# Clearing the sorted rows of a mixture of experts: only past each expert's last token, or all of them beforehand

## The chip, the cores and the metric

The kernel runs on one core of one Trainium2 chip. The metric is the time of one execution on the device in microseconds (us); the median of several runs is compared. One further execution was taken with the hardware profiler; the profile's views (page, waits, timeline, stretches of time) are all of that one execution.

## The reference, cut to what matters

The program is two layers, each an attention part and a feed-forward part, over x of 16 batch rows x 256 tokens x 256 features. Three quarters of the work (a conditioning attention, an attention of 16 heads, a quantized feed-forward, a diffusion step and a second attention) come first. The last part is a mixture of experts:

```
def _L1_ffn_ref(x, w_router, W1, b1, W2, b2, Ws1, bs1, Ws2, bs2):
    # D_MODEL 256, D_FF 1024, N_EXPERTS 8, TOP_K 2, one shared expert
    logits = einsum('btd,ed->bte', x, w_router)
    vals, idx = top_k(softmax(logits), 2)
    gates = sum(one_hot(idx, 8) * vals[..., None], axis=-2)
    acc = einsum('btf,df->btd', gelu(einsum('btd,fd->btf', x, Ws1) + bs1), Ws2) + bs2
    h = gelu(einsum('btd,efd->btef', x, W1) + b1)
    y = einsum('btef,edf->bted', h, W2) + b2
    return SCALE * (acc + einsum('bted,bte->btd', y, gates))

x = x + attention0(cross_attention(x, fside, braak_embed[stage]))
x = x + fp4_feed_forward(x @ W[category] + b[category])
x = x + attention1(diffusion(x, zX, zY, zR))
x = x + _L1_ffn_ref(conditioned(x, expert_of_row), ...)
```

Each of the 4096 tokens goes to 2 of 8 experts, so 8192 rows are to be worked on by experts, in numbers that are known only at run time.

## The kernel before, in words

**Two parts.** `program` runs `setup`, then `woven`, then `mixture`.

**The woven part** (0 to about 1720 us) holds everything up to the second attention. It is written as 22 generators, `stage_a`, `stage_f`, `stage_d` and so on, each of which yields the instructions of one kind of work for batch rows 0 to 15. `weave` is a planner: it keeps a modelled time at which each engine comes free, and again and again issues, of the next instructions of all generators, the one that could start first by the model (ties go by the ranks in `ORDER`). The order in which it issues is the order in which each engine works. An instruction on SyncE (its queue is where the transfers are issued) is booked with 0.5 us of that engine, and a transfer's data counts as there 1.5 us (`MOVED`, from on-chip memory) or 3.2 us (`LANDING`) later. The generators hold each other back through flags in `g.done`. `stage_f` does the feed-forward of layer 0 for batch row b and then sets `done["F"]` to b + 1; `stage_d`, the diffusion that opens the second attention for row b, waits for that flag (L1079), and `stage_e`, once all 16 are done, loads what the mixture needs first (`fetch_c`).

In the second attention the rotated queries and keys are made by VectorE and GpSimd (`turned4`, tiles `f_t1q` and `f_t1k`) and moved to other partitions by four small transfers each (`f_q<-f_t1q`, `keys<-f_t1k`, 64 KB) on SyncE; TensorE then takes the scores from `keys` and `f_q` (`scores4`). Weights are loaded by `fetch_p` (`wq`) and `fetch_u` (`wv`), the inputs of the next row by `fetch_a`, all on SyncE.

**The mixture.** `conditioned` works in blocks of 512 tokens. For each block `route` finds the two experts of each token and its place within each expert's region, and scatters the token's row into `ysort`, an array in HBM, with 8 indirect transfers on GpSimd (64 in all, L1531). Expert e owns the rows from e x REGION x 256 on. After the last block, `plan_tiles` counts the tokens of each expert (`pc`), rounds the counts up to tiles of 256 rows and makes a table of which tile belongs to which expert. Then four blocks of the shared expert run (`shared_block`), and after them 35 tiles of 256 sorted rows (`expert_tiles`), each of which reads its rows (`ys<-ysort`, L1392) and its expert's weights on SyncE. The last 4 of 39 tiles run only if the counts need them. `combine` gathers the results with indirect transfers.

**What the change touches.** A tile may reach past its expert's last token, and a spare tile may have no tokens at all. So that these rows hold numbers, before the change all of `ysort` (8 x 16 x 256 rows of 1 KB, 32 MB) is filled with zeros from the tile `zero`: after each batch row, `stage_f` yields two writes of 1 MB on SyncE, and only then sets its flag.

Of the kernel before, what the change touches and what calls it, by code (L numbers as in the profile page):

```python
# [12 lines left out]
F32 = mybir.dt.float32  # L13
I32 = mybir.dt.int32
BF16 = mybir.dt.bfloat16
AF = mybir.ActivationFunctionType
ALU = mybir.AluOpType
AX = mybir.AxisListType

P = 128  # L20
S = 256
D = 256
# [6 lines left out]
NE = 8  # L29
# [4 lines left out]
OUT_SCALE = 1.0 / math.sqrt(1 + TOPK / NE)  # L34
TT = 256
SPARE = NE // 2
REGION = 16
MAGIC = 1.5 * 2.0**22


# [4 lines left out]
def mm(nc, out, pairs, start=True, stop=True):  # L45

    last = len(pairs) - 1
    for i, (lhsT, rhs) in enumerate(pairs):
        nc.tensor.matmul(out, lhsT, rhs, start=start and i == 0, stop=stop and i == last)  # L49


def bank(k):

    return k.ps.tile([P, 512], F32, name=f"bank{k.stream}", tag=f"bank{k.stream}")
# [8 lines left out]
def setup(ctx, tc, a, n_batch):  # L63
    nc = tc.nc
    k = Ctx()
    k.nc, k.tc, k.a, k.B, k.turn, k.stream = nc, tc, a, n_batch, False, 0
    k.const = ctx.enter_context(tc.tile_pool(name="const", bufs=1))
    c = k.const
    k.ident = c.tile([P, P], F32, name="ident")
    make_identity(nc, k.ident)  # L70

    k.mask = c.tile([P, 2 * P], F32, name="mask")
    nc.gpsimd.memset(k.mask[:, :P], 0.0)
    make_causal_mask(nc, k.mask[:, P:], mask_val=NEG)

    k.idx = c.tile([64, 3, n_batch], I32, name="idx")
    k.onehot = c.tile([16, n_batch], F32, name="onehot")


    k.n_tiles = (TOPK * n_batch * S + NE * (TT - 1)) // TT  # L80
    dram = ctx.enter_context(tc.tile_pool(name="dram", bufs=1, space=bass.MemoryType.DRAM))
    k.ysort = dram.tile([NE * REGION * TT, D], F32, name="ysort")
    k.osort = dram.tile([k.n_tiles * TT, D], F32, name="osort")
    k.zero = c.tile([P, D], F32, name="zero")
    nc.gpsimd.memset(k.zero, 0.0)

    k.xd = [dram.tile([S, D], F32, name=f"xd{b}") for b in range(n_batch)]
    return k
# [670 lines left out]


def stage_f(g):
    k, a = g.k, g.a
    regions = NE * REGION * TT // (2 * g.B)
    for b in range(g.B):
        yield lambda b=b: g.done["Y"] > b
        yield from feed_forward0(g, b)

        for i in (2 * b, 2 * b + 1):
            rows = k.ysort[i * regions : (i + 1) * regions, :].rearrange("(p r) d -> p r d", p=P)
            yield g.sp.dma_start(out=rows, in_=k.zero.unsqueeze(1).to_broadcast([P, regions // P, D]))  # L770
        g.done["F"] = b + 1


# [604 lines left out]
def expert_rows(k, pool, r, t):  # L1378

    k.stream = t % 2  # L1380
    nc, a = k.nc, k.a

    own = k.p2.tile([P, 10], F32, name="own_b1", tag="own_b1")
    b1, entry = own[:, 0:8], own[:, 8:10].bitcast(I32)
    nc.vector.tensor_copy(b1, r.b1t[:, t, :])
    nc.vector.tensor_copy(entry, r.table[:, :, t])
    e = nc.sync.value_load(entry[0:1, 0:1], min_val=0, max_val=NE - 1)
    row = nc.sync.value_load(entry[0:1, 1:2], min_val=0, max_val=(NE * REGION - 1) * TT)
    w1 = pool.tile([P, 2, FF1], F32, name="w1", tag="w1")
    w2 = pool.tile([P, 8, D], F32, name="w2", tag="w2")  # L1390
    ys = k.p2.tile([P, 2, D], F32, name="ys", tag="ys")
    nc.sync.dma_start(out=ys, in_=k.ysort[bass.ds(row, TT), :].rearrange("(c p) d -> p c d", p=P))  # L1392
    nc.sync.dma_start(out=w1, in_=a["w1"][bass.ds(e, 1)].rearrange("e p c f -> p (e c) f"))
    nc.sync.dma_start(out=w2, in_=a["w2"][bass.ds(e, 1)].rearrange("e p f d -> p (e f) d"))
    b2 = k.p2.tile([P, D], F32, name="eb2", tag="eb2")
    nc.sync.dma_start(out=b2, in_=a["b2"][bass.ds(e, 1)].to_broadcast([P, D]))
    ysT = k.p2.tile([P, 2, TT], F32, name="ysT", tag="ysT")
    transposed(
        k,
        ysT.rearrange("p c (s t) -> p (c s) t", t=P),  # L1400
        [ys[:, s, c * P : (c + 1) * P] for c in range(2) for s in range(2)],
    )
    return ysT, w1, w2, b1, b2
# [46 lines left out]
def routing_state(k, keep):  # L1450
# [23 lines left out]
    for e in range(NE):  # L1474
        nc.gpsimd.memset(r.base[:, e : e + 1], float(e * REGION * TT))
    r.tri = keep.tile([P, NE, NE], F32, name="tri")
# [59 lines left out]
            )  # L1536


def plan_tiles(k, keep, r):

    nc = k.nc
    NT, n = 2 * k.B, k.n_tiles
    pc = bank(k)[:, :NE]
    mm(nc, pc, [(r.all, r.seen[:, NT, :])])
    cnt = keep.tile([P, NE], F32, name="cnt")
    ci = keep.tile([P, NE], I32, name="cnt_i")
    nc.vector.tensor_scalar(cnt, pc, float(TT - 1), None, ALU.add)
    nc.vector.tensor_copy(ci, cnt)
    nc.vector.tensor_scalar(ci, ci, TT.bit_length() - 1, None, ALU.arith_shift_right)
    nc.vector.tensor_copy(cnt, ci)  # L1550
    tmp = keep.tile([P, NE, NE], F32, name="pl_tmp")
    first = keep.tile([P, NE], F32, name="pl_first")
    end = keep.tile([P, NE], F32, name="pl_end")
    nc.vector.tensor_tensor(tmp, r.tri, cnt.unsqueeze(1).to_broadcast([P, NE, NE]), ALU.mult)
    nc.vector.tensor_reduce(first, tmp, AX.X, ALU.add)
    nc.vector.tensor_tensor(end, first, cnt, ALU.add)
    for t in range(n - SPARE, n):
        rows = k.osort[t * TT : (t + 1) * TT, :].rearrange("(c p) d -> p c d", p=P)
        nc.sync.dma_start(out=rows, in_=k.zero.unsqueeze(1).to_broadcast([P, 2, D]))
    r.used = keep.tile([P, 1], I32, name="pl_used")  # L1560
    nc.vector.tensor_copy(r.used, end[:, NE - 1 : NE])

    nc.gpsimd.memset(end[:, NE - 1 : NE], float(n))
    idx = keep.tile([P, n], I32, name="pl_idx")
    nc.gpsimd.iota(idx, pattern=[[1, n]], base=0, channel_multiplier=0)
    t_ = keep.tile([P, n], F32, name="pl_t")
    nc.vector.tensor_copy(t_, idx)
    wide = [P, n, NE]
    tw = t_.unsqueeze(2).to_broadcast(wide)
    ew = lambda x: x.unsqueeze(1).to_broadcast(wide)  # L1570
    hot = keep.tile(wide, F32, name="pl_hot")
    low = keep.tile(wide, F32, name="pl_low")
    nc.vector.tensor_tensor(hot, tw, ew(end), ALU.is_lt)
    nc.vector.tensor_tensor(low, tw, ew(first), ALU.is_ge)
    nc.vector.tensor_tensor(hot, hot, low, ALU.mult)
    ids = keep.tile([P, NE], I32, name="pl_ids")
    nc.gpsimd.iota(ids, pattern=[[1, NE]], base=0, channel_multiplier=0)
    idf = keep.tile([P, NE], F32, name="pl_idf")
    nc.vector.tensor_copy(idf, ids)
    tab = keep.tile([P, 2, n], F32, name="pl_tab")  # L1580
    nc.vector.tensor_tensor(low, hot, ew(idf), ALU.mult)
    nc.vector.tensor_reduce(tab[:, 0, :], low, AX.X, ALU.add)

    off = keep.tile([P, NE], F32, name="pl_off")
    nc.vector.scalar_tensor_tensor(off, first, -float(TT), r.base, ALU.mult, ALU.add)
    nc.vector.tensor_tensor(low, hot, ew(off), ALU.mult)
    nc.vector.tensor_reduce(tab[:, 1, :], low, AX.X, ALU.add)
    nc.vector.scalar_tensor_tensor(tab[:, 1, :], t_, float(TT), tab[:, 1, :], ALU.mult, ALU.add)
    nc.vector.tensor_scalar(tab[:, 1, :], tab[:, 1, :], float((NE * REGION - 1) * TT), None, ALU.min)
    r.table = keep.tile([P, 2, n], I32, name="pl_table")  # L1590
    nc.vector.tensor_copy(r.table, tab)

    r.b1t = keep.tile([P, n, 8], F32, name="b1t")
    part = keep.tile([P, n, 8], F32, name="b1part")
    for e in range(NE):
        h = hot[:, :, e : e + 1].to_broadcast([P, n, 8])
        dst = part if e else r.b1t
        nc.vector.tensor_tensor(dst, h, k.b1[:, e, :].unsqueeze(1).to_broadcast([P, n, 8]), ALU.mult)
        if e:
            nc.vector.tensor_tensor(r.b1t, r.b1t, part, ALU.add)  # L1600

    nc.vector.tensor_scalar(off, first, float(TT), None, ALU.mult)
    nc.vector.tensor_tensor(r.rank, r.rank, off.unsqueeze(1).to_broadcast([P, NT, NE]), ALU.add)
    pos = keep.tile([P, TOPK, NT], F32, name="pos_f")
    for i in range(TOPK):
        nc.vector.tensor_tensor(r.hot[:, i], r.hot[:, i], r.rank, ALU.mult)
        nc.vector.tensor_reduce(pos[:, i, :], r.hot[:, i], AX.X, ALU.add)
    r.pos_o = keep.tile([P, TOPK, NT], I32, name="pos_o")
    nc.vector.tensor_copy(r.pos_o, pos)
# [182 lines left out]
```

## Time and profile before

| | |
|---|---|
| median of 3 runs | 2716.26 us (2714.77 to 2721.61) |
| the profiled execution | 2712.26 us |
| its span, first to last instruction | 2710.5 us |
| granted TensorE clock, mean | 0.985 |
| TensorE / VectorE / ScalarE / GpSimd busy | 96% / 48% / 45% / 36% |
| zero writes, first and last issue | 186.5 and 1632.2 us |
| transfers in all | 303.59 MB |

Engines are PE (TensorE), PEld (its weight load), DVE (VectorE), ACT (ScalarE), POOL (GpSimd) and SP (SyncE; SPq is its queue). In a timeline row stand the start, the duration, engine, line, operation, output and inputs, the number of instructions merged, and in brackets the idle time before it with what ended that. Every instruction of the woven part carries line L181, so there it is told apart by its tiles. In rows on a stretch of time stand the stretch, its length, the busy time of PE, PEld, DVE, ACT and POOL with instruction counts, the granted clock, the share of the 16 DMA engines that was busy, and GB/s.

### The profile page before, as it was taken

The numbers are of one execution on the slowest core, as the hardware profiler recorded it, in microseconds if no ns is written. First come the engines' busy times: TensorE is split into PE (matmuls) and PEld (weight loads), VectorE is DVE, ScalarE is ACT, GpSimd is POOL, SyncE is SP. The second block draws the span as 40 slices with busy tenths as digits, with TensorE's granted clock in tenths as the row PEclk, the third lists the DMA queues.
The fourth block names the chain that finished last, engine by engine and source line by source line (L and its number), as shares of the span: only waits on it lengthen the run. The fifth ranks groups of instructions, "written<-read, shape, count | busy, mean of one in ns | idle before, by whom it ended". The sixth has DMA issues, their size and how long they took to land. (4 is left out here: it accounts for less than half of the span.)

```text
span 2710.5 us, 39421 instructions
## 1 busy us (share of the span) xinstructions
PE 2593.2 (96%) x13569; PEld 1902.7 (70%) x13569; DVE 1310.9 (48%) x2557; ACT 1211.4 (45%) x3618; POOL 988.4 (36%) x1022
## 2 busy tenths in 40 slices
PE   8988999999999999999999998999999999999999
PEld 7755666766766666676776676555566888888866
DVE  6466666666677755766667664234330000000023
ACT  2554636655565654655655643333322222222321
POOL 5344544545555544554545543233320000000045
PEclk9999999999999998999999999999999999999999
DMA  4121233333333233233242336411120555655523
GB/s 123 52 87 50 90 115 114 93 117 108 94 111 109 67 113 115 69 118 124 80 124 89 89 114 185 135 52 47 49 103 1 185 195 192 204 186 192 194 86 109
DMA packets 249657, 303.59 MB, mean 112 GB/s; under 512 B 43120, under 2 KB 216432, under 8 KB 240112
## 3 DMA queue, kind: packets, MB, share of 16 engines
q1 hardware_dynamic: 243312, 284.26, 33.4%
q0 software_dynamic: 6144, 16.79, 2.0%
q8 instruction: 110, 1.80, 0.3%
q14 instruction: 91, 0.75, 0.1%
HBM read 206.85 MB, written 60.56 MB: 99 GB/s over the span
## 5 line engine op out<-in xcount | busy, mean ns | idle before, releaser
L181 PE MATMUL single<-e_zT,wq 128*128 128x256 f32 x1024 | 288.6, 403 | 8.3 <-DMA wq<-in_w_qk 7.5
L1436 POOL DMA_INDIRECT got<-osort,pos_o x64 | 62.2, 972 | 626.5 <-ACT hT L1369 584.9
L1418 ACT ACTIVATE ehT<-bank,own_b 128x256 f32<-128x256 f32 x280 | 132.5, 473 | 349.1 <-PE bank L49 349.1
L181 POOL TENSOR_TENSOR b_e<-b_e,b_stat 128x512 f32<-128x512 f32 (+1 forms) x128 | 189.7, 1483 | 179.1 <-DVE b_stat L181 167.4
L49 PE MATMUL bank<-ysT,w 128*128 128x256 f32 x1120 | 247.6, 379 | 0.2 <-ACT ysT L105 0.2
L49 PE MATMUL bank<-w,ehT 128*128 128x256 f32 x1120 | 247.5, 379 | 0.0
L49 PEld LDWEIGHTS bank<-ysT,w 128*128 128x128 f32 x1120 | 212.7, 190 | 29.4 <-ACT ysT L105 0.5
L49 PEld LDWEIGHTS bank<-w,ehT 128*128 128x128 f32 x1120 | 210.2, 190 | 27.2
L181 ACT ACTIVATE b_e<-b_e,b_stat 128x128 f32<-128x128 f32 (+1 forms) x512 | 227.0, 447 | 0.9 <-DVE b_stat L181 0.9
L181 PEld LDWEIGHTS single<-e_zT,wq 128*128 128x128 f32 x1024 | 178.8, 193 | 50.6 <-issue 15.2
L181 ACT ACTIVATE f_prob<-f_prob,f_stat 128x144 f32<-128x144 f32 x512 | 207.5, 410 | 12.1 <-DVE f_stat L181 12.1
L181 ACT COPY b_pT<-single 128x512 f32<-128x512 f32 x190 | 108.8, 588 | 138.2 <-PE single L181 137.4
L181 PE MATMUL pair<-keys,f_q 64*128 64x144 f32 x1024 | 126.8, 334 | 16.6 <-DMA keys<-f_t1k 13.1
L1426 DVE TENSOR_TENSOR eo<-bank,eb 128x512 f32<-128x512 f32 x35 | 24.2, 691 | 234.4 <-PE bank L49 234.4
L181 PE MATMUL single<-wv,e_zT 128*128 128x256 f32 x512 | 134.1, 386 | 2.7 <-DMA wv<-in_w_v 1.4
L181 PE MATMUL single<-wo,f_oT 128*128 128x256 f32 x512 | 131.4, 383 | 3.5 <-ACT f_oT L181 3.3
L181 PEld LDWEIGHTS pair<-keys,f_q 64*128 64x128 f32 x1024 | 77.0, 188 | 81.7 <-issue 60.8
L181 ACT COPY f_pT<-single 128x512 f32<-128x512 f32 x130 | 76.0, 588 | 122.9 <-PE single L181 120.4
L181 POOL TENSOR_TENSOR f_t1q<-f_t1q,f_t2q 128x256 f32<-128x256 f32 x128 | 93.0, 746 | 96.6 <-DVE f_t2q L181 65.1
L181 POOL TENSOR_TENSOR f_prob<-f_prob,f_stat 128x1024 f32<-128x1024 f32 x64 | 127.2, 1987 | 0.1
L181 PE MATMUL single<-ident,b_e 128*128 128x128 f32 x768 | 119.9, 285 | 7.2 <-POOL b_e L181 4.2
L1531 POOL DMA_INDIRECT ysort<-r_y,r_posi x64 | 62.4, 975 | 162.2 <-DMA ysort<-r_y,r_posi 103.6
(299 smaller groups left out, 5324.9 us busy)
## 6 DMA issues: line engine op xcount, KB each, us to landing
w<-in_w SPq DMA_DIRECT2D x70, 1024.0 KB, 5.3
wq<-in_w_qk SPq DMA_DIRECT2D x128, 256.0 KB, 3.3
ysort<-zero SPq DMA_DIRECT2D x32, 1024.0 KB, 7.3
wv<-in_w_v SPq DMA_DIRECT2D x64, 256.0 KB, 3.6
f_q<-f_t1q SPq DMA_DIRECT2D x256, 64.0 KB, 2.0
keys<-f_t1k SPq DMA_DIRECT2D x256, 64.0 KB, 2.1
wo<-in_w_out SPq DMA_DIRECT2D x64, 256.0 KB, 3.1
ys<-ysort SPq DMA_DIRECT2D x35, 256.0 KB, 2.7
```

The costliest lines, as they stand in the source:

```text
L49: nc.tensor.matmul(out, lhsT, rhs, start=start and i == 0, stop=stop and i == last)
L181: return Op([(self.name, self.cost(fn, outs, aps), lambda: call(*args, **kw))], outs, aps)
L1418: nc.scalar.activation(hT[:, f, :], ph, AF.Gelu_apprx_tanh, bias=b1[:, f : f + 1])
L1426: nc.vector.tensor_tensor(o, po, b2.unsqueeze(1).to_broadcast([P, 2, D]), ALU.add)
L1436: nc.gpsimd.indirect_dma_start(out=g, out_offset=None, in_=k.osort[:, :], in_offset=bass.IndirectOffsetOnAxis(ap=r.pos_o[:, i, t : t + 1], ...
L1531: nc.gpsimd.indirect_dma_start(out=k.ysort[:, :], out_offset=bass.IndirectOffsetOnAxis(ap=posi[:, i, t : t + 1], axis=0), in_=ys[t], in_of ...
```

## The change

The two writes per batch row in `stage_f` go, and `done["F"]` is set right after the feed-forward. In `plan_tiles`, as soon as the counts `pc` are there, the new `blank_rows` adds each expert's count to the start of its region, loads the eight sums into registers of SyncE one after the other, and from each of these rows on writes 256 rows of zeros (for the last expert 1024 rows). REGION grows from 16 to 17 and `ysort` gets 3 x 256 rows behind the last region, so that the writes stay inside; the bound on a tile's first row follows.

```diff
-REGION = 16
+REGION = 17
+PAST = 3
...
-    k.ysort = dram.tile([NE * REGION * TT, D], F32, name="ysort")
+    k.ysort = dram.tile([(NE * REGION + PAST) * TT, D], F32, name="ysort")
...
 def stage_f(g):
     k, a = g.k, g.a
-    regions = NE * REGION * TT // (2 * g.B)
     for b in range(g.B):
         yield lambda b=b: g.done["Y"] > b
         yield from feed_forward0(g, b)
-
-        for i in (2 * b, 2 * b + 1):
-            rows = k.ysort[i * regions : (i + 1) * regions, :].rearrange("(p r) d -> p r d", p=P)
-            yield g.sp.dma_start(out=rows, in_=k.zero.unsqueeze(1).to_broadcast([P, regions // P, D]))
         g.done["F"] = b + 1
...
-    row = nc.sync.value_load(entry[0:1, 1:2], min_val=0, max_val=(NE * REGION - 1) * TT)
+    row = nc.sync.value_load(entry[0:1, 1:2], min_val=0, max_val=(NE * REGION + PAST - 1) * TT)
...
+def blank_rows(k, keep, r, counts):
+
+    nc = k.nc
+    ends, endi = keep.tile([P, NE], F32, name="ends"), keep.tile([P, NE], I32, name="ends_i")
+    nc.vector.tensor_tensor(ends, counts, r.base, ALU.add)
+    nc.vector.tensor_copy(endi, ends)
+    for e in range(NE):
+        base, n = e * REGION * TT, TT + PAST * TT * (e == NE - 1)
+        row = nc.sync.value_load(endi[0:1, e : e + 1], min_val=base, max_val=base + (REGION - 1) * TT)
+        rows = k.ysort[bass.ds(row, n), :].rearrange("(p r) d -> p r d", p=P)
+        nc.sync.dma_start(out=rows, in_=k.zero.unsqueeze(1).to_broadcast([P, n // P, D]))
...
 def plan_tiles(k, keep, r):
...
     ci = keep.tile([P, NE], I32, name="cnt_i")
+    blank_rows(k, keep, r, pc)
     nc.vector.tensor_scalar(cnt, pc, float(TT - 1), None, ALU.add)
...
-    nc.vector.tensor_scalar(tab[:, 1, :], tab[:, 1, :], float((NE * REGION - 1) * TT), None, ALU.min)
+    nc.vector.tensor_scalar(tab[:, 1, :], tab[:, 1, :], float((NE * REGION + PAST - 1) * TT), None, ALU.min)
```

## The prediction, made before the change was run

> **What bounds the kernel now.** I read the page first, then who TensorE waited for, then the stretches of time in which the 32 writes run, and last the place where the new writes will stand.
>
> ```profile
> span 2710.5 us, 39421 instructions
> PE 2593.2 (96%) x13569; PEld 1902.7 (70%) x13569; DVE 1310.9 (48%) x2557; ACT 1211.4 (45%) x3618; POOL 988.4 (36%) x1022
> ysort<-zero SPq DMA_DIRECT2D x32, 1024.0 KB, 7.3
> keys<-f_t1k SPq DMA_DIRECT2D x256, 64.0 KB, 2.1
> ```
>
> TensorE is busy for 96% of the span and nothing else for half of it, so time can be won only where TensorE stands still or runs at a lower clock. The writes to be removed are 1 MB each, 32 times. The small moves of rotated keys, 64 KB each, share their queue.
>
> The waits of TensorE alone, longest first in total (who, for what: us, times, longest):
>
> ```profile
> PE pair L181 <- DMA keys<-f_t1k: 13.1, 4, 4.0
> PE single L181 <- DMA wq<-in_w_qk: 7.5, 1, 7.5
> PE pair L181 <- DMA wq<-in_w_qk: 3.4, 1, 3.4
> ```
>
> Only four of 256 key moves were waited for, and the timeline puts those waits at 362.3, 963.0, 1068.9 and 1273.6 us, each 7.7 to 10.3 us after the second of a pair of zero writes was issued. The queue of SyncE around the third of them:
>
> ```profile
> 1059.90 0.62 SPq L181 DMA_DIRECT2D keys<-f_t1k  x1
> 1060.57 1.32 SPq L181 DMA_DIRECT2D ysort<-zero  x2
> 1061.99 4.23 SPq L181 DMA_DIRECT2D keys<-f_t1k  x3
> 1066.32 2.29 SPq L181 DMA_DIRECT2D wq<-in_w_qk  x2
> ```
>
> Ahead of the pair an issue takes 0.62 us; behind it three take 4.23 us, 1.4 us each, and in this stretch the DMA view gives the keys 5.8 us to landing instead of 2.1. On TensorE:
>
> ```profile
> 1064.75 0.60 PE L181 MATMUL single<-e_zT,wq 128*128 128x256 f32 x2
> 1065.19 0.60 PE L181 MATMUL single<-ident,b_e 128*128 128x128 f32 x4
> 1068.93 0.52 PE L181 MATMUL pair<-keys,f_q 64*128 64x144 f32 x4 [3.15 <-DMA keys<-f_t1k]
> 1069.38 1.22 PE L181 MATMUL single<-e_zT,wq 128*128 128x256 f32 x2
> ```
>
> It waits 3.15 us, and then the same two matmuls take 1.22 us where they took 0.60. The stretches behind the waits, with the granted clock in the third column from the right, show why:
>
> ```profile
> 362.78:366.19 3.41, 3.41 (x12) 2.21 (x11) 2.40 (x4) 0.00 (x0) 1.06 (x1) 0.50 0.71 226
> 963.52:966.94 3.42, 3.42 (x12) 2.08 (x12) 1.56 (x5) 0.99 (x3) 1.66 (x3) 0.50 1.03 350
> 1069.34:1076.16 6.82, 6.82 (x22) 4.27 (x21) 1.65 (x5) 1.39 (x5) 1.75 (x3) 0.50 0.93 287
> 1274.14:1277.55 3.41, 3.41 (x5) 1.35 (x5) 0.00 (x0) 0.00 (x0) 0.00 (x0) 0.50 0.82 251
> 1646.19:1653.02 6.83, 3.52 (x8) 2.87 (x9) 0.00 (x0) 0.00 (x0) 0.00 (x0) 0.50 0.85 216
> ```
>
> After each of the waits the clock stands at 0.50 for 3.4 or 6.8 us. So such a wait costs itself and then half of the slow stretch.
>
> **Part one: the 32 writes leave the woven part.** Two writes per batch row go, each 0.66 us of SyncE's queue (21 us in all) and 1 MB of traffic. The queue time by itself is worth nothing, since SyncE is not the bound. What counts is who stood behind them.
>
> The four key waits: 3.12 + 2.83 + 3.15 + 3.99 = 13.1 us. Would the keys be in time without the pair? Third wait: GpSimd made the last of their rows at 1058.7 + 0.7 = 1059.4, the three issues would start at 1060.57, end at 1062.5, and land 2.1 us after the last began, at 1064.0; TensorE wanted them at 1065.8. The same working gives 1268.4 against 1269.6 for the fourth, 358.0 against 359.2 for the first and 955.8 against 960.1 for the second. All four vanish if the order stays.
>
> The slow clock behind them: 3.41 + 3.42 + 6.82 + 3.41 = 17.1 us at 0.50, so 8.5 us. The Trainium skill ("TensorE: Matmul & The Clock Gate", Part 1: The HAM clock gate) lets the clock fall to half after at least one idle window of about 3.4 us. By that rule three of these waits, at about 3 us, would leave the clock alone, and the gain would be 6.8 us smaller; the trace disagrees and shows 0.50 behind each.
>
> The last pair, at 1631.6, stands ahead of eight loads for the next stage, and then of the `wq` that TensorE waits 7.53 us for (until 1649.50); of the slow stretch there 3.52 us are worked, which costs 1.8. The gain lies between 0 (the eight loads clog the queue by themselves) and 9.3 us (the pair's 2 MB take about 8 us at the 260 to 300 GB/s of the other pairs' stretches). I take half, 4.6.
>
> Sum with the order kept: 13.1 + 8.5 + 4.6 = 26.2 us, at most 30.9.
>
> But the order won't be kept. `weave` books 0.5 us of SyncE for each of these writes, and `stage_f` sets `done["F"]`, which releases `stage_d`, only after them. Without them later DMAs are booked up to 1 us earlier, and the greedy choice goes another way from 187 us on. Between 200 and 1720 us TensorE's waits add up to 75.3 us, of which the zero writes explain 13.1 + 7.5; the other 55 us get drawn again. The 200 us stretches from 400 to 1600 us have 5.7 to 9.4 us without TensorE work, so a redraw moves one by 2 us or so either way, and all eight, if independent, by about 5. I set 4 us of the gain aside for it, because a TensorE that is held up less reaches the next late operand of ScalarE or GpSimd sooner. That leaves 22 us.
>
> **Part two: eight writes in `plan_tiles`.** Two VectorE operations on 128x8, like L1547's 0.15 us, enter at 1991 us. TensorE is then in 14 us of matmuls from 1997.7 and waits for no result of the plan, so they cost nothing; uncovered they would cost 0.3 us. SyncE gets eight register loads, each about 0.58 us by the reads of L1387 (0.27 for the load, 0.15 and 0.02 for what follows, the rest between them), and eight writes: seven of 256 KB and one of 1 MB. The skill ("DMA: Bandwidth & Descriptors", Latency and other measured facts) gives such a load a floor of about 600 ns; the trace shows 0.27, and by the page's figure SyncE would be busy some 2.6 us longer.
>
> The writes must wait for the last scatter, which the read of tile 0 already does:
>
> ```profile
> 2015.48 0.41 SPq L1392 DMA_DIRECT2D ys<-ysort  x1
> 2093.98 1.01 PEld L99 LDWEIGHTS bank<-ident,ys 128*128 128x128 f32 x8
> ```
>
> Queued behind them on SyncE are that read and the expert weights of tiles 0 and 1. TensorE meanwhile has shared blocks until 2094, 78 us of cover. If the eight don't wait for each other, SyncE needs 8 x (0.58 + 0.66) = 10 us and the last lands 5 to 12 us later: the read goes out near 2033. If each waits for the one before it, with 2.7 us to landing for 256 KB (the clearing of `osort`) and 7.3 for 1 MB, it is 7 x 3.3 + 7.9 = 31 us, so near 2047. The weights follow in 5 us and take at most 14.4 to land: 2067. Either way the cover holds and the price is 0. If it failed, each us beyond would stop TensorE. The scatters wait for each other (103.6 us of GpSimd) before and after; the clamp and the region size are constants and cost nothing.
>
> **The rivals.**
> - *The new order costs more than the writes did* (slower). Place: the woven part, 187 to 1720 us. One fresh wait there has a row: at 475.6, far from any zero write, TensorE waits 3.4 us for a move and 3.41 us at 0.50 follow, 5.1 us together. The gain of 26.2 turns into a loss of over 8.1 us with seven such places: 2716.3 - 26.2 + 36 = 2726. For it: the trace has five half-clock stretches between 400 and 1730 us that no zero write explains, so a worse draw is possible. Against: it would have to more than double them, while SyncE is relieved.
> - *Other bursts take the writes' place* (no change). The five loads of `fetch_a` and three of `fetch_p` and `fetch_u` also crowd the queue; if they hold up the keys in most places, only a sixth of the gain stays: 2712. Against: outside the pairs keys land in 2.1 us.
> - *The eight writes outlast their cover.* At 11.7 us to landing, the longest of any zero write, and chained: 8 x 12.4 = 99 us, the read at 2115 and landed at 2117, 23 us after 2094, and about 2 us of slow clock: 2716.3 - 22 + 25 = 2719. It decides from a read issued after about 2091. Against: the 11.7 was seen with a full queue; here it is empty.
> - That the change doesn't do what it says I can rule out: the writes are out of `stage_f`, and nothing else issues them.
>
> **How the numbers follow.** The profiled execution took 2712.26 us (span 2710.5, 1.8 around it), 4.0 below the median of 2716.26. Less 22 that is 2690.3, and 2694.3 beside the median. The forecast's own range is 2684 to 2706, from the full 30.9 with a slightly lucky order to half the gain; chance 0.62. Other bursts 0.16 and the outlasted cover 0.04, both within 0.3% (8 us, about what a measurement of this kernel can tell from no change); a costly order 0.18. The range reaches from 2682 to 2724, which leaves out some luck below and half of the slower case.
>
> **What would show it.** Right: no wait of TensorE for `keys` over 2 us within 12 us of a burst; the granted clock up from 0.985 to about 0.99; TensorE's idle time between 200 and 1700 us down from 76 us to below 62; the first `ys` read between 2030 and 2050 and TensorE without a gap at 2094. Wrong: idle time there of 76 us or more, or a gap of several us ahead of the first tile.

## The result and the profile after

| | median | range | ratio to before, 95% interval |
|---|---|---|---|
| before | 2716.95 us | 2714.77 to 2721.61 | |
| after | 2698.48 us | 2692.99 to 2699.43 | 0.9926 [0.9907, 0.9944] |

The change saves 18.5 us, 0.7%. The forecast was 2694.3 us, 22 less than before.

The page of the kernel after, its row of the key moves (the last figure is the median time from issue to landing), and the rows of the eight register loads and the eight writes in the views of their lines (durations in ns: least, median, most; first and last start; all lines of the code have moved by one or more):

```profile
span 2697.0 us, 39427 instructions
PE 2593.9 (96%) x13569; PEld 1904.9 (71%) x13569; DVE 1313.4 (49%) x2559; ACT 1211.3 (45%) x3618; POOL 987.0 (37%) x1022
keys<-f_t1k SPq DMA_DIRECT2D x256, 64.0 KB, 2.1
L1542 SPq TENSOR_LOAD <-ends_i x8: 262/267/442, 1978.3 to 1982.5; - x8
L1544 SPq DMA_DIRECT2D ysort<-zero x8: 541/542/684, 2001.9 to 2007.2; - x8
```

Span less busy time is the time in which TensorE stood still: 117.3 us before, 103.1 after. That is 14.2 less, with the same busy time, 2593.2 and 2593.9. The waits of TensorE in the kernel after:

```profile
PE pair L182 <- DMA own<-in_fc2c: 4.4, 1, 4.4
PE single L182 <- DMA wq<-in_w_qk: 2.3, 2, 1.4
```

No line names `keys` any more, where before they stood for 13.1 us. The one wait of 7.5 us for `wq` is gone too. Behind the eight loads of the mixture, where it stood, TensorE now waits 4.4 us for an operand of the scores (the two short waits for `wq` come 12 and 20 us later):

```profile
1621.56 0.73 PE L182 MATMUL pair<-keys,f_q 64*128 64x144 f32 x4 [4.37 <-DMA own<-in_fc2c]
```

The view names the last of the loads, which landed at 1621.28. But the matmul reads `keys` and `f_q`, and the last move of `f_q`, issued behind the loads from 1616.11 to 1619.00, landed at 1621.46, just ahead of it. The place where the eight writes stand, on SyncE and then on TensorE:

```profile
2001.94 5.83 SPq L1544 DMA_DIRECT2D ysort<-zero  x8
2012.53 0.41 SPq L1387 DMA_DIRECT2D ys<-ysort  x1
```
```profile
2069.65 11.17 PE L50 MATMUL bank<-w2s,hT 128*128 128x256 f32 x51
2080.66 1.04 PE L100 MATMUL bank<-ident,ys 128*128 128x128 f32 x8
```

The eight go out in one row, 0.76 us apart on average, while one takes 2.6 us to land (median), so none waits for another; the first read of `ys` follows 10.6 us after the first of them, and TensorE passes from the shared blocks to the first tile (2080.66) without a gap. From there to the end both kernels take 616.3 us, so all of the gain lies ahead of the experts.

### The profile page after: what moved, and what is told of

Same layout as the page of the kernel before. It is cut to its first block, busy times and chain, and to the rows that moved or that the text cites. A ratio compares the mean times of both kernels' runs of the same rounds, so it can differ in the third digit from the quotient of the medians.

```text
span 2697.0 us, 39427 instructions
## 1 busy us (share of the span) xinstructions
PE 2593.9 (96%) x13569; PEld 1904.9 (71%) x13569; DVE 1313.4 (49%) x2559; ACT 1211.3 (45%) x3618; POOL 987.0 (37%) x1022
## 5 line engine op out<-in xcount | busy, mean ns | idle before, releaser
L182 DVE TENSOR_TENSOR x<-x,single 128x512 f32<-128x512 f32 (+1 forms) x112 | 67.5, 604 | 124.9 <-PE single L182 124.9
L182 DVE TENSOR_TENSOR f_prob<-pair,mask 128x576 f32<-128x576 f32 x128 | 95.2, 746 | 56.9 <-PE pair L182 56.6
```

Source lines behind the costliest of these rows:

```text
L182: return Op([(self.name, self.cost(fn, outs, aps), lambda: call(*args, **kw))], outs, aps)
```

## The experiments

**The order kept, the writes gone.** After, with this in `stage_f`:

```diff
         yield from feed_forward0(g, b)
+        for i in range(2):
+            op = g.sp.dma_start(out=g.k.ysort[0 : 8 * P, :], in_=g.k.zero.unsqueeze(1))
+            op.choices = [(*op.choices[0][:2], lambda: None)]
+            yield op
         g.done["F"] = b + 1
```

> The kernel after, but the planner still books the two SyncE slots per batch row and the flag still waits for them; nothing is issued in them. Every engine's order in the woven part is that of the kernel before, only the 32 writes are missing. Theory (the writes' traffic holds up the small moves behind them): the four key waits (13.1 us) and the slow clock behind them (8.5) vanish and the wait for wq at 1649 shrinks (about 4.6), so some 2691 us beside 2717, at worst 2700. Rival (the planner's new order is the luckier one, the writes were hidden): 2714 to 2720. No TensorE wait for keys by the theory, four by the rival.

2689.25 us, 0.9891 [0.9877, 0.9906]: 28.7 us below the 2717.97 of its before. Its page:

```profile
span 2683.9 us, 39439 instructions
PE 2586.5 (96%) x13569; PEld 1902.2 (71%) x13569; DVE 1310.3 (49%) x2559; ACT 1211.4 (45%) x3618; POOL 988.7 (37%) x1022
```

TensorE stands still for 97.4 us, 19.9 less than before. The four key waits, 13.1 us, are gone, and of the 7.53 us for `wq` behind the eight loads 1.55 are left at the same place:

```profile
1623.99 1.96 PE L182 MATMUL single<-e_zT,wq 128*128 128x256 f32 x8 [1.55 <-DMA wq<-in_w_qk]
```

TensorE's busy time falls by 6.7 us for the same matmuls, which is the clock. From 200 to 1730 us the stretches at 0.50 add up to 61.4 us before and 47.8 here; half the difference is 6.8. All five stretches behind the writes are gone (23.9 us), and one of 6.8 us near 1021; but 17 us elsewhere, near 322, 469, 650 and 763 us, are new or have grown.

The matmuls of the third key wait, in the timeline of this kernel, with nothing standing still between them:

```profile
1057.38 0.60 PE L182 MATMUL single<-e_zT,wq 128*128 128x256 f32 x2
1057.81 0.60 PE L182 MATMUL single<-ident,b_e 128*128 128x128 f32 x4
1058.34 0.52 PE L182 MATMUL pair<-keys,f_q 64*128 64x144 f32 x4
1058.79 0.70 PE L182 MATMUL single<-e_zT,wq 128*128 128x256 f32 x2
```

Before, the `keys` matmul in this row stood 3.15 us, and the two after it took 1.22 us. The rival that the order did it is out: with the order of before the gain is larger than with the new one.

**The writes kept, in the new order.** Before, with the writes issued past the planner:

```diff
-            yield g.sp.dma_start(out=rows, in_=k.zero.unsqueeze(1).to_broadcast([P, regions // P, D]))
+            k.nc.sync.dma_start(out=rows, in_=k.zero.unsqueeze(1).to_broadcast([P, regions // P, D]))
```

> The kernel before, but its 32 writes are issued without being booked by the planner. Every compute engine's order in the woven part is that of the kernel after, and the 32 writes stand in SyncE's queue at the ends of the same feed-forwards; no writes in plan_tiles. Theory: key waits come back behind the pairs, in other places than before, 10 to 20 us with their slow clock: 2708 to 2720. Rival (order): 2695 to 2701, as the kernel after.

2721.47 us, 1.0012 [1.0000, 1.0023], a little above the range given: a miss. Its waits of TensorE:

```profile
PE pair L181 <- DMA keys<-f_t1k: 9.5, 3, 4.0
PE pair L181 <- DMA f_q<-f_t1q: 9.2, 1, 9.2
```

The key waits are back, three of them. The 9.2 us are the place where the last pair and the eight loads for the mixture stand in one row on SyncE, and one of the moves of the queries (64 KB) behind them:

```profile
1623.47 1.32 SPq L770 DMA_DIRECT2D ysort<-zero  x2
1624.84 3.77 SPq L181 DMA_DIRECT2D x<-xd  x2
...
1632.03 2.81 SPq L181 DMA_DIRECT2D own<-in_fc2c  x2
1634.88 2.97 SPq L181 DMA_DIRECT2D f_q<-f_t1q  x1
```

The two runs and the two kernels make a square. The traces bear it out: in the woven part every engine works in the same order in this run as in the kernel after, and in the first run as in the kernel before. Between the two kernels the order is the same up to 1065 us, but for 16 matmuls near 360 us, so the planner drew another one only for the last 650 us. Taking the writes out gives 28.7 us in the old order and 2721.5 - 2698.5 = 23 us in the new one. The new order costs 3.5 us with the writes and 2698.5 - 2689.3 = 9 us without (10 if each is taken against its own before, as these differ by 1 us).

**Bytes or issues.** As the first run, but each booked slot issues a write of 32 KB:

```diff
-            op.choices = [(*op.choices[0][:2], lambda: None)]
+            small = lambda i=i: g.k.nc.sync.dma_start(out=g.k.ysort[i * P : (i + 1) * P, 0:64], in_=g.k.zero[:, 0:64])
+            op.choices = [(*op.choices[0][:2], small)]
```

> As e1_order_kept (order of the kernel before, eight writes in plan_tiles), but in each booked slot a write is issued, of 32 KB instead of 1 MB: the 32 issues on SyncE are back, their bytes are not. If the bytes in the queue held up the keys, the time stays with e1_order_kept: 2686 to 2694 and no wait for keys. If the 0.66 us that an issue holds SyncE did it, most of the 29 us is lost again: 2705 to 2717.

2692.29 us, 0.9909 [0.9892, 0.9926]. The 32 issues are in the trace:

```profile
L768 SPq DMA_DIRECT2D ysort<-zero x32: 422/446/607, 187.4 to 1613.0; - x32
```

No wait for `keys` comes back, and most of the gain stays. The interval overlaps that of the first run, so whether the issues alone cost 3 us isn't settled; what the writes carry costs the rest. Bytes and packets are not told apart: the page counts 249657 packets before, 223930 here and 219323 in the first run.

**The eight writes without their cover.** After and before, each with the shared blocks moved behind the expert tiles:

```diff
+        expert_tiles(k, ew, r, range(k.n_tiles - SPARE))
         for blk in range(early):
             k.stream = blk % 2
             shared_block(k, r, w1s, w2s, blk)
-        expert_tiles(k, ew, r, range(k.n_tiles - SPARE))
```

> The kernel after with its four early shared blocks moved behind the expert tiles, so that nothing covers the eight writes: the first expert tile follows the plan at once. If the eight writes cost SyncE 10.6 us (2001.94 to 2012.53 in the trace of after) they show here in full: this kernel against the next one of this call stands some 18 - 11 = 7 to 8 us lower, not 18. If the cover had been needless, the distance stays 18.

> The kernel before with the same four shared blocks moved behind the expert tiles. TensorE then waits for the scatters and for the first weights, from about 1998 to 2024, with slow clock behind it: about 2717 + 26 + 2 = 2745. Only its distance to the kernel of the run before matters.

2747.57 us, 1.0112 [1.0094, 1.0129], for the kernel after; 2757.65 us, 1.0136 [1.0117, 1.0155], for the one before: 10.1 us between them, where 18.5 lie between the covered pair and 7 to 8 were expected. The 10.1 are rough, as the four times of the first spread over 16 us; the waits below are firmer. The kernel before without cover was expected at 2745, a miss by 12.7: beside the wait below, TensorE also stood still for 5.8 us until an operand of the router (`r_sel`) and for 3.1 us until the first weights, and its busy time rose by 7.6 us. TensorE's wait for the rows of the first tile, in the first of them and in the second:

```profile
PE bank L100 <- DMA ys<-ysort: 37.6, 1, 37.6
```
```profile
PE bank L99 <- DMA ys<-ysort: 27.1, 1, 27.1
```

10.5 us more: the price of the eight writes when nothing lies beside them, and the same as the 10.6 us on SyncE. In the kernel after the shared blocks hide it all.

**Other orders, the same work.** As the first run, with one, three and four empty slots booked per batch row (`range(1)`, `range(3)`, `range(4)`).

> As e1_order_kept, with one empty SyncE slot of 0.5 us booked per batch row instead of two. Same work, another order drawn by the planner. If the 9 us between e1_order_kept (two slots) and the kernel after (none) are the luck of an order, this lies anywhere within some 10 us of them: 2685 to 2707. If fewer booked slots are worse in themselves, it lies between the two, 2690 to 2697.

> As e1_order_kept, with three empty slots per batch row. Luck of the order: 2685 to 2707. If more booked slots are better in themselves: under 2689.

> As e1_order_kept, with four empty slots per batch row. Luck of the order: 2685 to 2707. If more booked slots are better in themselves: under e7_three_slots.

| slots booked | median | ratio, 95% interval |
|---|---|---|
| none (the kernel after) | 2698.48 us | 0.9926 [0.9907, 0.9944] |
| one | 2689.63 us | 0.9900 [0.9884, 0.9916] |
| two (the first run) | 2689.25 us | 0.9891 [0.9877, 0.9906] |
| three | 2693.42 us | 0.9916 [0.9901, 0.9931] |
| four | 2698.14 us | 0.9930 [0.9915, 0.9946] |

Five orders of one work lie within 9 us. One slot takes as long as two and not something between none and two, and three and four aren't better, so the time doesn't follow the number. The kernel after drew one of the two slowest. In the profiles TensorE stands still for 103.1, 100.7, 97.4, 103.2 and 104.2 us, in the order of the table. Small waits for `keys` come up in some of these orders with no large write near: with three slots there are three, 3.8 us together and 1.7 at most.

**The last burst spread.** After, with three groups of the mixture's loads held back by one block of scores each:

```diff
+    def later():
+        n = min(g.done["S"] + 1, 4 * g.B)
+        return lambda: g.done["S"] >= n
...
+    yield later()
     yield from get("fc1", [P, 2, FF1], a["fc1"])
...
+    yield later()
     yield from get("fc2", [P, 8, P], a["fc2a"])
...
+    yield later()
     for i in range(2):
```

> The kernel after, but three groups of the mixture's first loads (fc1; fc2 and wr; own) are each held back until one more block of scores is done; before, all eight loads are issued in one go at 1609 us. The order changes only from there on. If bytes ahead of the small moves are what costs, TensorE's wait of 4.4 us at 1621 in the kernel after and the slow clock behind it go: 2692 to 2695 beside 2698.5. If that wait had another cause, 2698 stays.

2699.11 us, 0.9928 [0.9914, 0.9941]: no gain, a miss. SyncE and TensorE after the edit:

```profile
1619.59 0.58 SPq L182 DMA_DIRECT2D fc<-in_fc  x1
...
1621.24 1.76 SPq L182 DMA_DIRECT2D f_q<-f_t1q  x3
```
```profile
1626.20 1.54 PE L182 MATMUL pair<-keys,f_q 64*128 64x144 f32 x16 [2.89 <-DMA f_q<-f_t1q]
```

The wait has moved: 2.9 us for three moves of `f_q` that now stand behind `fc1`, 1 MB. At this place a gap between the loads didn't help, since the small moves were issued right behind one of them.

> The same spreading on e1_order_kept, whose trace has no such wait. Theory: nothing to win, 2686 to 2693.

2686.20 us, 0.9890 [0.9875, 0.9905], as expected the same as the first run. Of all versions measured, these two and the one with a single slot are the fastest.

> The kernel after, unchanged, beside the two others on one chip: 2698.5 within 4 us.

2697.97 us, 0.9928 [0.9914, 0.9941]. Its page, and the stretch from 762 to 772 us in the profile after and then in this one:

```profile
span 2689.0 us, 39427 instructions
PE 2585.4 (96%) x13569; PEld 1898.2 (71%) x13569; DVE 1313.0 (49%) x2559; ACT 1211.2 (45%) x3618; POOL 987.0 (37%) x1022
```
```profile
762.00:772.00 10.00, 8.81 (x44) 5.22 (x45) 8.14 (x17) 5.56 (x21) 6.72 (x6) 0.83 0.49 150
```
```profile
762.00:772.00 10.00, 9.06 (x50) 5.66 (x47) 7.05 (x17) 3.94 (x16) 6.13 (x7) 1.00 0.41 126
```

The same kernel stood still for the same time, 103.6 us against 103.1, but was busy for 8.5 us less. In the first profile a slow stretch lies in this window (clock 0.83), in the second none at this place (1.00). So the clock's share of a difference can't be read from one profile on each side.

## Why the prediction was right, point by point

- *The key waits, 13.1 us.* Right. All four vanish, in the old order and in the new one, and in the new order three come back when the writes do.
- *The slow clock, 8.5 us behind them and 1.8 behind `wq`.* Right in kind: the stretches behind the writes went. But others came, so TensorE's busy time fell by 6.7 us with the order kept and by 7.8 in the second profile of the kernel after, and rose by 0.7 in the first. The working counted only what goes and had not allowed for the 8.5 us by which two executions of one kernel differ; that the net comes near its 10.3 us is partly luck.
- *The wait for `wq`, 4.6 of at most 9.3.* Too small for the kept order, where 6.0 of the 7.5 us and the slow stretch of 1.8 went, 7.8 together. In the new order the other end of the bound came nearly true: behind the same eight loads 4.4 us were lost, to a move of the queries. The second rival, that other bursts take the writes' place, holds at this one place.
- *The sum with the order kept, 26.2 us and at most 30.9.* 28.7 by the medians, 26.6 by the spans of the two profiles.
- *4 us set aside for the order.* The term that was mis-sized: 9 to 10 us without the writes. It was taken from how much the 200 us stretches differ, with all eight redrawn from 187 us on; in fact the order of the kernel after differs only from 1065 us on, but for 16 matmuls. Five orders show a spread of 9 us, and the kernel after lies at its upper end. The slower rival was this mechanism, and it did act; its price was put at 36 us and was 9 to 10. Where they come from is known in part: 5.7 us are TensorE's idle time (103.1 against 97.4), half of that behind the eight loads (4.4 against 1.6), yet spreading these won nothing. The rest is busy time, which one profile of each doesn't settle.
- *The forecast, 22 us less.* That it came within 4 us of the 18.5 is partly luck: with the order kept 2.5 us more were won than in the sum, and the new order cost some 6 more than was set aside.
- *The eight writes cost nothing.* Right, and shown by taking the cover away. Their time on SyncE was estimated at 17 to 31 us until the read goes out; it was 10.6. The eight register loads ran from 1978.3 to 1983.0, ahead of the last scatter, which was issued at 1999.5, and so took no time behind it; the seven small writes landed by 2009.3, before the large one, which landed at 2012.25, just ahead of the read.
- *The signs to look for.* No wait for `keys`: seen. No gap at the first tile: seen. Idle time of TensorE between 200 and 1700 us under 62 us: not seen, it came to 66, 4.4 of it the new wait, and to 63 with the order kept. Clock near 0.99: 0.986 in one profile and 0.989 in the other. The read of `ys` between 2030 and 2050: not seen, it was at 2012.5.

## What to carry to other kernels

A large transfer that nobody waits for is not free when small, late-made moves share its queue: look for the small ones that land late, and for the slow clock behind each wait. Where a planner or a greedy order decides, a change of the work also redraws the order; booking the old slots and leaving them empty separates the two, and here the empty slots were worth 9 us by themselves, by the luck of the draw. Before zeros are moved onto a path, find what will lie beside them, and check it once by taking that cover away.

## What was not expected of the hardware

The granted clock fell to 0.50 for different times in two executions of the same kernel with the same idle time. Six stretches are the same in both; two, near 652 and 1502 us, last 6.8 us in one and 3.4 in the other, and two, near 765 and 1707 us, are missing in the other. From 200 to 1730 us they add up to 58.0 us in one and 41.0 us in the other, worth 8.5 us by TensorE's busy time, nearly half of what the change brought. The Trainium skill ("TensorE: Matmul & The Clock Gate", Part 1: The HAM clock gate) says that the window in which activity is judged runs freely; that would let one wait tip the clock in one execution and not in the next, and these two profiles agree with it. In each, the slow stretches begin whole multiples of 3.413 us apart, the length of the shortest: the four that begin at 293.9 to 652.3 us in the first are 30.72, 146.77 and 180.91 us apart, which is 9, 43 and 53 times that. The same page's idle window of about 3.4 us doesn't fit the stretch near 765 us: no wait longer than 1.4 us lies within the 9 us ahead of it.
